# Set-up and experts' copies of a fused convolution, attention and mixture-of-experts kernel: the third norm's roots on VectorE, weights loaded by SyncE, copies paced

## The chip, the cores and the metric

The kernel runs on one core of a Trainium2 chip. The metric is the device time of one execution in microseconds (us), here as the median of three runs. The engines are named PE (TensorE), DVE (VectorE), ACT (ScalarE), POOL (GpSimd) and SP (SyncE, which issues DMAs and computes nothing). Each engine takes its instructions in order and waits on semaphores; DMAs are issued by SP, ACT or POOL and run beside them.

## The reference

The input x has 8 images of 56x56 positions with 256 channels. A convolution layer of 32 paths comes first, then an attention layer over the positions of each image, then a mixture of 8 experts of which each token uses two.

```python
def path(x, w1, b1, ..., v3):                    # 32 of these, each with D = 4 inner channels
    h = relu(bn(x @ w1 + b1, g1, be1, m1, v1))   # 256 -> 4
    h = conv3x3(h, w2, padding="SAME") + b2      # 4 -> 4
    h = relu(bn(h, g2, be2, m2, v2))
    h = h @ w3 + b3                              # 4 -> 256
    return relu(bn(h, g3, be3, m3, v3))          # bn: g * (h - m) * rsqrt(v + 0.001) + b

x = relu(sum(path(x, *w) for w in weights) + x)
t = tokens(x)
t = t + attention(layernorm(t))                  # 8 heads, linear in the keys and values
n = layernorm(t)
y = n
for e in range(8):                               # weights: softmax over the router, best two
    y = y + weight[:, e] * (gelu(n @ w1[e] + b1[e]) @ w2[e] + b2[e])
t = t + y
```

The change concerns the constants `g3`, `b3`, `m3`, `v3`, `be3` of the third norm, the 3x3 weights `W2`, and the copies of `w1`, `b1`, `w2` of the experts.

## The kernel before, in words

**Chunks and slots.** The 3136 positions of each image are cut into 7 chunks of 448 (`CH`), 56 chunks in all (`S`). The main loop runs over slots. In slot s TensorE computes the third convolution (`conv3_steps`, L625) of chunk s; beside it stand the first convolution of chunk s+2 (`conv1_steps`: transposes `tx` of the chunk's input `xi` at L260, then products with `W1s` at L271, then ACT writes `h1`), the 3x3 convolution of chunk s+1 (`spread_taps` copies shifted rows of `h1` into `R`, `conv2_steps` multiplies them with `W2t` at L307 and splits the result into `hi` and `lo`, which DMAs interleave into the tile `hl`), the layer norm of chunk s-1 (`end_steps`), and, from slot 8 on, the attention, routing and expert tiles of earlier chunks. `hl` has two buffers, `xi` has one.

**Order.** For PE, ACT and DVE the order of instructions is written out by hand: each part of a slot is a list of steps with weights or places between 0 and 1, and `issue` sorts all steps of a slot by place. conv3 gives 32 pairs of products in 16 steps of weight 0.7 and 8 sums of weight 0.9, spread over the whole slot. SP and POOL are not in that list: a scheduler puts their instructions in the order in which it expects them to become ready. A DMA of SP with nothing to wait for is so moved to the front of the program.

**Pacing.** `pair` keeps its latest product in `pace`. The scatters of rows (POOL) are given a dependency on `pace[0]`, that is on the last pair of conv3 that was placed before them, so that they are spread over the slot.

**The set-up.** Before slot 0 the constants are loaded and rearranged. `path_rows` loads each of the third norm's five vectors as a tile of 128 partitions x 64. POOL raises `v3` + 0.001 to the power -0.5 (L209). DVE makes the factor `g3` and the offset `b3`. `whole` copies each of them by four DMAs into a tile of 32 x 256, alternating between the queues of ACT and SP (L196). TensorE spreads `g3` over 128 partitions with the matrix `spread` (L373, `tp_g`), DVE multiplies `W3s` by it, four pairs of products (L380, L381, `tp_w`) place the result in `W3hl`, and `bias3` becomes `b3t` through L409 (`tp_b`). ACT loads `W2s` by 12 DMAs (L217), from which DVE makes `W2t`. Two chunks of conv1 and the first chunk of conv2 are computed among this. For chunk 0, ACT issues one of the three DMAs of `R` (L294) and the two of `hl` that take `lo` (L329).

**The experts' copies.** `copy_weights(e)` gathers the weights of expert e in a DRAM tensor `Wd` (three DMAs: two of 256 KB at L488 and a small one at L494), and `empty_rows(e)` writes an empty tile `pad` of 259 KB to the head of the expert's part of each of two DRAM tensors `regions` (L1296; POOL clears the tile at L1294). Both are called in slots 1 to 8, at the places 0.5 and 0.8:

```python
if 1 <= s <= E:
    work_of.append((0.5, 0.5, [(0.0, lambda: copy_weights(s - 1))]))
    work_of.append((0.8, 0.8, [(0.0, lambda: empty_rows(s - 1))]))
```

They depend on nothing that the slots compute, and SP's order places them where it will.

Of the kernel before, what the change touches and what calls it, by code (L numbers as in the profile page):

```python
# [8 lines left out]
F32 = mybir.dt.float32  # L9
BF16 = mybir.dt.bfloat16  # L10
I32 = mybir.dt.int32
F32R = mybir.dt.float32r
AF = mybir.ActivationFunctionType
ALU = mybir.AluOpType
# [7 lines left out]
SYNC = mybir.DependencyInfo(mybir.DependencyClass.Sync, mybir.DependencyReason.DATA)  # L22
# [3 lines left out]
def kernel(  # L26
# [24 lines left out]
    nc = tc.nc  # L51
    B, N, C = x.shape
# [6 lines left out]
    P = 128  # L59
    NF = C // P  # L60
# [36 lines left out]
    setup = setup_pool.__enter__()  # L97
# [10 lines left out]
    for g in range(NG):  # L108
        nc.scalar.dma_start(
            out=bn2s[32 * g : 32 * g + 32],  # L110
            in_=bn2[32 * g : 32 * g + 32].rearrange("(a e) k -> e a k", a=4),
# [24 lines left out]
    def group_mask(t, groups, size, value):  # L136

        nc.gpsimd.memset(t, value)
        nc.gpsimd.affine_select(
            out=t, in_=t, compare_op=ALU.is_ge, fill=0.0, base=0,  # L140
            pattern=[[-size, groups], [0, t.shape[2]]], channel_multiplier=1,
        )
        nc.gpsimd.affine_select(
            out=t, in_=t, compare_op=ALU.is_ge, fill=0.0, base=size - 1,
            pattern=[[size, groups], [0, t.shape[2]]], channel_multiplier=-1,
        )
# [34 lines left out]
        gather, ident.rearrange("q (p c) -> q c p", c=32), AX.X, ALU.add  # L181
    )


    CQ = C // 4

    def path_rows(src, name):
        t = setup.tile([P, CQ], F32, name=name)
        nc.sync.dma_start(out=t, in_=src.rearrange("p (q c) -> (p q) c", q=4))
        return t  # L190

    def whole(parts_of, name):
        t = setup.tile([NP, C], F32, name=name)
        for q in range(4):
            queue = nc.sync if q % 2 else nc.scalar
            queue.dma_start(out=t[:, q * CQ : (q + 1) * CQ], in_=parts_of[q : P : 4, :])  # L196
        return t

    v3 = path_rows(V3, "v3")
    g3 = path_rows(G3, "g3q")  # L200
    b3 = path_rows(B3, "b3q")
    m3 = path_rows(M3, "m3")
    be3 = path_rows(Be3, "be3")
    W3s = setup.tile([P, C], F32, name="W3s")
    nc.sync.dma_start(out=W3s, in_=W3.rearrange("p d c -> (p d) c"))
    nc.vector.tensor_scalar_add(v3, v3, BN_EPS)
    mhalf3 = setup.tile([P, CQ], F32, name="mhalf3")
    nc.gpsimd.memset(mhalf3, -0.5)
    nc.gpsimd.tensor_tensor(v3, v3, mhalf3, ALU.pow)  # L209


    path32 = setup.tile([P, GP, D], F32, name="path32")
# [1 line left out]
    W2s = setup.tile([3 * 32, NG, 3, D], F32, name="W2s")  # L214
    for dx in range(3):
        for g in range(NG):
            nc.scalar.dma_start(  # L217
                out=W2s[dx : 3 * 32 : 3, g],
                in_=W2[32 * g : 32 * g + 32].rearrange(
                    "q (dy dx o) -> dx q dy o", dy=3, dx=3  # L220
                )[dx],
            )
# [117 lines left out]

    path_mask = setup.tile([P, NP, D], F32, name="path_mask")
    group_mask(path_mask, NP, D, 1.0)
    nc.vector.tensor_mul(g3, g3, v3)
    nc.vector.tensor_sub(b3, b3, m3)
    nc.vector.tensor_mul(b3, b3, g3)
    nc.vector.tensor_add(b3, b3, be3)
    g3 = whole(g3, "g3")
    bias3 = whole(b3, "bias3")

    picks = setup.tile([P, 2, NQ, P], F32, name="picks")  # L350
    nc.gpsimd.memset(picks, 0.0)
# [18 lines left out]
    spread = setup.tile([NP, P], F32, name="spread")  # L370
# [112 lines left out]
    NTOK = B * N  # L483
    M = 2 * E + 1

    def copy_weights(e):
        for n, w in enumerate((w1, w2)):
            nc.sync.dma_start(  # L488
                out=Wd[e, :, n * NF * C : (n + 1) * NF * C].rearrange(
                    "p (f h) -> p f h", f=NF  # L490
                ),
                in_=w[e].rearrange("(f p) h -> p f h", p=P),
            )
        nc.sync.dma_start(out=Wd[e, :, 2 * NF * C :], in_=b1T[:, e * NF : (e + 1) * NF])  # L494

    regions = [
        tc.dram_tile([E * CAPR, ROW], F32, name=f"regions_{k}") for k in range(2)
# [1 line left out]
    Wd = tc.dram_tile([E, P, WROW], F32, name="Wd")  # L499
# [42 lines left out]
    for e in range(M):  # L542
# [6 lines left out]
        out=below, in_=below, compare_op=ALU.is_ge, fill=0.0, base=-1,  # L549
# [8 lines left out]
        out=earlier, in_=earlier, compare_op=ALU.is_ge, fill=0.0, base=-1,  # L558
# [13 lines left out]
    def unordered(ins, group, keep=()):  # L572

        tc.declare_no_dep(ins, group=group, keep=keep, reason="other rows")
# [95 lines left out]

    spilled, rs1s, kvs = {}, {}, {}
    G = KT * NH

    def inverse_root(v, y, h):

        nc.vector.tensor_scalar(y, v.bitcast(I32), 1, None, ALU.arith_shift_right)
        nc.vector.tensor_scalar(y, y, -1, 0x5F3759DF, ALU.mult, ALU.add)
        y = y.bitcast(F32)
        for _ in range(3):
            nc.vector.scalar_tensor_tensor(h, y, -0.5, v, op0=ALU.mult, op1=ALU.mult)  # L680
            nc.vector.tensor_mul(h, h, y)
            nc.vector.scalar_tensor_tensor(y, h, 1.5, y, op0=ALU.add, op1=ALU.mult)
        return y

    def end_steps(s):
        b, c = divmod(s, NCH)
# [58 lines left out]
        def variances():  # L745
# [28 lines left out]
            y = stat.tile([T, KT, NH + 1], I32, tag="root1", name=f"root1_{s}", bufs=1)  # L774
            h = stat.tile([T, KT, NH + 1], F32, tag="root2", name=f"root2_{s}", bufs=1)
            y = v["y"] = inverse_root(sd, y, h)
            nc.vector.tensor_mul(sd, sd, y)

# [133 lines left out]
    def attn_steps(a):  # L912
# [15 lines left out]
        def attend(k):  # L928

            ps = ps_mm.tile([T, C + 2 * E], F32, tag="mm", name=f"at_{a}_{k}")  # L930
            for f in range(NF):
                nc.tensor.matmul(  # L932
                    ps, tT[:, f, k * T : (k + 1) * T], tables_of[b][:, f, :],
                    start=(f == 0), stop=(f == NF - 1),
                )
            nc.vector.scalar_tensor_tensor(
                X[:, k, :], ps[:, :C], rs1[:, k : k + 1], X[:, k, :],
                op0=ALU.mult, op1=ALU.add,
            )
            late.append(lambda: nc.scalar.copy(lg[:, k, :], ps[:, C:]))  # L940
            if k:
                late.pop(0)()
            nc.vector.bn_stats(st[:, k, :], X[:, k, :])
            nc.vector.bn_aggr(mv[:, k, :], st[:, k, :])
            if k == KT - 1:
                nc.vector.tensor_scalar_add(rs2, mv[:, :, 1], LN_EPS)
                if alone:
                    y, h = (
                        stat.tile(
                            [T, KT, NH + 1], dt, tag=f"root{n}", name=f"root{n}_{a}_a", bufs=1  # L950
                        )[:, :, 0]
                        for n, dt in ((1, I32), (2, F32))
                    )
                    nc.vector.tensor_copy(rs2, inverse_root(rs2, y, h))
                else:
                    nc.gpsimd.tensor_tensor(rs2, rs2, mhalf[:T, :KT], ALU.pow)
# [43 lines left out]
    pace = []  # L1000
    before = {}

    def filled(b, ins):
        unordered(ins, "rows")
        unordered(ins, "tiles")
        tc.add_to_no_dep_group("rows", ins)
        before.setdefault(b, []).append(ins)
# [131 lines left out]
    def plan_steps(b):  # L1139
# [17 lines left out]
        def small(shape, tag, dtype=F32):  # L1157
            whole = [P, 2] + [NMAX if d == n else M if d == m else d for d in shape]
            if tag == "big":
                whole[2] = max(NMAX, M)  # L1160
            t = tables.tile(whole, dtype, tag=f"p_{tag}", name=f"{tag}_{b}")
            return t[tuple(slice(0, d) for d in [P, 2] + shape)]
# [129 lines left out]
    def empty_rows(e):  # L1292
        pad = slots.tile([P, 2, ROW], F32, tag="rows", name=f"pad_{e}", bufs=5)
        nc.gpsimd.memset(pad, 0.0)  # L1294
        for k in range(2):
            ins = nc.sync.dma_start(  # L1296
                out=regions[k][e * CAPR : e * CAPR + TR, :].rearrange("(h p) c -> p h c", p=P),
                in_=pad,
            ).ins
            filled(0, ins)  # L1300

    def take_rows(i):
# [185 lines left out]
    for s in range(S + A + 1):  # L1488
# [48 lines left out]
# [3 lines that stand above are left out]
# [65 lines left out]
```

## Time and profile before

| | |
|---|---|
| median of 3 runs | 3205.17 us (3203.22 to 3205.35) |
| the profiled execution's own time | 3181.84 us |
| its span in the profile | 3180.0 us |
| granted PE clock, mean | 0.964 |
| busy: PE, DVE, ACT, POOL | 2922.0, 2176.6, 1915.4, 1855.4 us |
| first product of conv3 (L625) | at 60.8 us |
| first pad and last pad issued by SP | at 24.9 and 75.5 us |
| DMAs of `Wd` issued by SP | at 13.5 to 72.6 us |

The span is the time between the first and the last instruction of one execution; the chain up to the first product of conv3 can be read in the timeline, where each row has the start, the duration, the engine (SPq and ACTq are the queues in which SP and ACT issue DMAs), the line, the operation with output and inputs, the count of merged instructions and, in brackets, the idle time before it and what ended it. Tile names stand without their numbers: `g<-g3q` is the DMA that fills the whole `g3`, `v` is `v3`, `h` is `h1` or `h2`, `c` any of the convolutions' results.

### The profile page before, as it was taken

Reading aid. Unit: us, or ns where it says so; the run is one execution under the profiler, and the core shown is the slowest. Engines: PE = TensorE matmul, PEld = TensorE weight load, DVE = VectorE, ACT = ScalarE, POOL = GpSimd, SP = SyncE. Lnnn points to the kernel's source line nnn. Section 1 sums busy time; section 2 is a strip of 40 time slices with the busy share of each in tenths; the row PEclk is TensorE's granted clock in tenths of the full one; section 3 lists DMA queues with packets and bytes.
Section 4 is the critical chain, followed back from the end, with each engine's and each line's share of the span. In section 5 each row is a group of like instructions: output and inputs, shape, how many; then the busy total and the mean of one; then the engine's idle time right before and its main releaser. Section 6 shows DMA issues by size and latency. Waiting matters only on the chain. (4 is left out here: it accounts for less than half of the span.)

```text
span 3180.0 us, 53655 instructions
## 1 busy us (share of the span) xinstructions
PE 2922.0 (92%) x16677; PEld 1664.3 (52%) x16677; DVE 2176.6 (68%) x5732; ACT 1915.4 (60%) x3827; POOL 1855.4 (58%) x1365
## 2 busy tenths in 40 slices
PE   5999888888999999999999999999999998898798
PEld 2333434334455555555555555555555545776687
DVE  3778877787878777776878687776777785444100
ACT  2676665555665666566666666566666664454355
POOL 3223254545566666757666675756764546677777
PEclk8999988898999999999999999999999999899999
DMA  8332343354456677566766667577665766898897
GB/s 173 117 108 83 104 130 116 113 152 149 135 161 187 161 196 194 162 178 186 195 170 174 189 174 194 158 185 196 173 191 152 193 164 169 189 265 219 200 228 179
DMA packets 322669, 537.53 MB, mean 169 GB/s; under 512 B 41152, under 2 KB 232784, under 8 KB 322384
## 3 DMA queue, kind: packets, MB, share of 16 engines
q1 hardware_dynamic: 238272, 429.85, 45.0%
q0 software_dynamic: 81984, 103.45, 17.8%
q8 instruction: 133, 2.18, 0.3%
q14 instruction: 152, 1.25, 0.1%
q10 hardware_dynamic: 2128, 0.81, 0.1%
HBM read 248.01 MB, written 192.55 MB: 139 GB/s over the span
## 5 line engine op out<-in xcount | busy, mean ns | idle before, releaser
L633 DVE SCALAR_TENSOR_TENSOR r<-c,nb,r 128x448 f32<-128x448 f32 x1792 | 1130.6, 676 | 433.1 <-ACT r L630 431.4
L630 ACT ACTIVATE r<-c,b3t 128x448 f32<-128x448 f32 x1792 | 1039.3, 635 | 338.9 <-PE c L625 333.4
L1405 POOL DMA_INDIRECT out_dram<-y,index x420 | 660.8, 1573 | 326.8 <-ACT y L1391 207.5
L625 PE MATMUL c<-hl,W3hl 64*128 64x448 f32 x3584 | 693.5, 429 | 48.2 <-ACT r L630 18.9
L1113 POOL DMA_INDIRECT regions<-pay,rrowi x448 | 429.2, 958 | 311.3 <-PE c L625 209.7
L646 PE MATMUL su<-r,gather 128*32 128x448 f32 x3584 | 554.6, 566 | 41.5 <-DVE r L633 38.6
L625 PEld LDWEIGHTS c<-hl,W3hl 64*128 64x128 f32 x3584 | 328.8, 189 | 480.6 <-issue 232.1
L1391 ACT ACTIVATE y<-py,rows 128x256 f32<-128x256 f32 x420 | 195.9, 475 | 471.8 <-PE py L1387 360.9
L1367 PE MATMUL ph<-eT,w 128*128 128x256 f32 x1680 | 451.3, 400 | 20.0 <-DMA w<-Wd 7.3
L1387 PE MATMUL py<-w,hT 128*128 128x256 f32 x1680 | 432.2, 382 | 0.0
L1367 PEld LDWEIGHTS ph<-eT,w 128*128 128x128 f32 x1680 | 304.6, 195 | 151.0 <-issue 50.9
L770 POOL TENSOR_TENSOR hsd<-hsd,half 112x36 f32<-112x36 f32 x49 | 304.5, 6215 | 67.1 <-DVE hsd L768 66.2
L1371 ACT ACTIVATE hT<-ph,w 128x256 f32<-128x256 f32 x420 | 197.1, 478 | 211.7 <-PE ph L1367 157.3
L1387 PEld LDWEIGHTS py<-w,hT 128*128 128x128 f32 x1680 | 291.6, 192 | 28.6
L932 PE MATMUL at<-tab,tT 128*112 128x272 f32 x896 | 262.7, 417 | 8.7 <-ACT r L630 6.6
L731 POOL TENSOR_TENSOR norm<-t,hmean 112x512 f32<-112x512 f32 x112 | 121.5, 1164 | 226.1 <-PE c L625 156.8
L646 PEld LDWEIGHTS su<-r,gather 128*32 128x32 f32 x3584 | 101.0, 109 | 245.2 <-DVE r L633 120.6
L1383 PE MATMUL py<-b2hl,own 128*128 128x256 f32 x420 | 179.4, 427 | 23.5 <-ACT y L1391 17.1
L932 PEld LDWEIGHTS at<-tab,tT 128*112 128x112 f32 x896 | 149.6, 181 | 86.4 <-issue 21.4
L1058 POOL TENSOR_TENSOR rq<-ebase,rq 112x8 f32<-112x8 f32 (+1 forms) x32 | 50.3, 1572 | 229.5 <-DVE rq L1057 229.1
L1383 PEld LDWEIGHTS py<-b2hl,own 128*128 128x128 f32 x420 | 79.7, 190 | 157.4 <-issue 45.2
L307 PE MATMUL c<-R,W2t 96*32 96x448 f32 x1344 | 149.9, 553 | 4.5 <-ACT r L630 4.5
(259 smaller groups left out, 3179.9 us busy)
## 6 DMA issues: line engine op xcount, KB each, us to landing
w<-Wd SPq DMA_DIRECT2D x210, 513.0 KB
rows<-regions SPq DMA_DIRECT2D x210, 259.0 KB
xi<-in_x_dram SPq DMA_DIRECT2D x56, 448.0 KB
hl<-hi SPq DMA_DIRECT2D x112, 224.0 KB
tTs<-u SPq DMA_DIRECT2D x56, 448.0 KB
ts<-t SPq DMA_DIRECT2D x56, 448.0 KB
tT<-tTs SPq DMA_DIRECT2D x56, 448.0 KB
X<-ts SPq DMA_DIRECT2D x56, 448.0 KB
```

The source lines that it names most:

```text
L625: product = nc.tensor.matmul(tiles[g][:, :CH], W3hl[rows, ab, cg, :], hl[rows, ab, :], start=True, stop=True)
L630: nc.scalar.activation(r, tiles[0][:, :CH], AF.Relu, bias=b3t[:, cg, 2 * ab : 2 * ab + 1])
L633: nc.vector.scalar_tensor_tensor(r, tiles[1][:, :CH], nb3[:, cg, 2 * ab + 1 : 2 * ab + 2], r, op0=ALU.max, op1=ALU.add,)
L646: nc.tensor.matmul(ps[32 * c4 : 32 * c4 + 32, :CH], gather, unit.pop((s, 4 * u + c4)), start=(ab == 0), stop=(ab == NQ - 1),)
L770: nc.gpsimd.tensor_tensor(sd, sd, half[:T, :].rearrange("q (k h) -> q k h", k=KT), ALU.pow)
L932: nc.tensor.matmul(ps, tT[:, f, k * T : (k + 1) * T], tables_of[b][:, f, :], start=(f == 0), stop=(f == NF - 1),)
L1113: ins = nc.gpsimd.indirect_dma_start(out=regions[n], out_offset=bass.IndirectOffsetOnAxis(ap=v["row_i"][:, (m - group[0]) * KT + k, n : n ...
L1367: nc.tensor.matmul(ps, w[:, f * C + hf * P : f * C + (hf + 1) * P], eT[:, f, :], start=(f == 0), stop=(f == NF - 1),)
L1371: nc.scalar.activation(hT[:, hf, :], ps, AF.Gelu, bias=w[:, 2 * NF * C + hf : 2 * NF * C + hf + 1])
L1383: nc.tensor.matmul(ps, own.to_broadcast([P, P]), b2hl, start=True, stop=False)
L1387: nc.tensor.matmul(ps, hT[:, f, h * P : (h + 1) * P], w[:, (NF + f) * C : (NF + f + 1) * C], start=False, stop=(f == NF - 1),)
L1405: ins = nc.gpsimd.indirect_dma_start(out=out_rows, out_offset=at, in_=y[:, h, :], in_offset=None, compute_op=ALU.add, **partial,).ins
```

## The change

- The root of the third norm is computed on DVE by `inverse_root`, which takes a first guess from the bits of the number and three Newton steps, 11 operations; the function stood further down and is moved up. The `pow` on POOL and its tile of exponents are gone.
- The four operations that make `g3` and `b3`, and the calls of `whole`, stand directly behind the root, not behind conv1 of the first two chunks.
- The DMAs of `whole` and of `W2s` are all issued by SP.
- The three DMAs of `copy_weights` and the two of `empty_rows` get a dependency on `pace[0]`, so SP issues them in the slots in which they are called.

```diff
@@ set-up
     def whole(parts_of, name):
         t = setup.tile([NP, C], F32, name=name)
         for q in range(4):
-            queue = nc.sync if q % 2 else nc.scalar
-            queue.dma_start(out=t[:, q * CQ : (q + 1) * CQ], in_=parts_of[q : P : 4, :])
+            nc.sync.dma_start(out=t[:, q * CQ : (q + 1) * CQ], in_=parts_of[q : P : 4, :])
         return t
...
     nc.vector.tensor_scalar_add(v3, v3, BN_EPS)
-    mhalf3 = setup.tile([P, CQ], F32, name="mhalf3")
-    nc.gpsimd.memset(mhalf3, -0.5)
-    nc.gpsimd.tensor_tensor(v3, v3, mhalf3, ALU.pow)
+    v3 = inverse_root(
+        v3, setup.tile([P, CQ], I32, name="root3"), setup.tile([P, CQ], F32, name="rest3")
+    )
+    nc.vector.tensor_mul(g3, g3, v3)
+    nc.vector.tensor_sub(b3, b3, m3)
+    nc.vector.tensor_mul(b3, b3, g3)
+    nc.vector.tensor_add(b3, b3, be3)
+    g3 = whole(g3, "g3")
+    bias3 = whole(b3, "bias3")
...
     for dx in range(3):
         for g in range(NG):
-            nc.scalar.dma_start(
+            nc.sync.dma_start(
                 out=W2s[dx : 3 * 32 : 3, g],
...
     path_mask = setup.tile([P, NP, D], F32, name="path_mask")
     group_mask(path_mask, NP, D, 1.0)
-    nc.vector.tensor_mul(g3, g3, v3)
-    nc.vector.tensor_sub(b3, b3, m3)
-    nc.vector.tensor_mul(b3, b3, g3)
-    nc.vector.tensor_add(b3, b3, be3)
-    g3 = whole(g3, "g3")
-    bias3 = whole(b3, "bias3")
@@ the experts' copies
+    def paced(ins):
+
+        tc.add_manual_dep(ins, pace[0].name, SYNC, reason="spread over the slot")
+        return ins
+
     def copy_weights(e):
         for n, w in enumerate((w1, w2)):
-            nc.sync.dma_start(
+            load = nc.sync.dma_start(
                 out=Wd[e, :, n * NF * C : (n + 1) * NF * C].rearrange(
...
-        nc.sync.dma_start(out=Wd[e, :, 2 * NF * C :], in_=b1T[:, e * NF : (e + 1) * NF])
+            paced(load.ins)
+        paced(
+            nc.sync.dma_start(out=Wd[e, :, 2 * NF * C :], in_=b1T[:, e * NF : (e + 1) * NF]).ins
+        )
@@ empty_rows
             ).ins
+            paced(ins)
             filled(0, ins)
```

The function that is moved up:

```python
def inverse_root(v, y, h):
    nc.vector.tensor_scalar(y, v.bitcast(I32), 1, None, ALU.arith_shift_right)
    nc.vector.tensor_scalar(y, y, -1, 0x5F3759DF, ALU.mult, ALU.add)
    y = y.bitcast(F32)
    for _ in range(3):
        nc.vector.scalar_tensor_tensor(h, y, -0.5, v, op0=ALU.mult, op1=ALU.mult)
        nc.vector.tensor_mul(h, h, y)
        nc.vector.scalar_tensor_tensor(y, h, 1.5, y, op0=ALU.add, op1=ALU.mult)
    return y
```

The order of instructions that follows: PE's is the same throughout, ACT loses 16 DMA issues, DVE gains 11 operations, and SP's differs only up to slot 8.

More of the change, by code (lines that the diff above doesn't have):

```diff
@@ L182, with inverse_root @@
     )
+    def inverse_root(v, y, h):
+        nc.vector.tensor_scalar(y, v.bitcast(I32), 1, None, ALU.arith_shift_right)
+        nc.vector.tensor_scalar(y, y, -1, 0x5F3759DF, ALU.mult, ALU.add)
+        y = y.bitcast(F32)
+        for _ in range(3):
+            nc.vector.scalar_tensor_tensor(h, y, -0.5, v, op0=ALU.mult, op1=ALU.mult)
+            nc.vector.tensor_mul(h, h, y)
+            nc.vector.scalar_tensor_tensor(y, h, 1.5, y, op0=ALU.add, op1=ALU.mult)
+        return y
     CQ = C // 4
@@ L672 @@
     G = KT * NH
[L674 to L683, printed above, removed]
     def end_steps(s):
```

## The prediction

> **What bounds the kernel now.** I read the page first (busy shares, slices), then the stage table of the first 100 us, then the timeline of the set-up and of one slot. The page gives 3180.0 us:
>
> ```profile
> PE   5999888888999999999999999999999998898798
> DMA  8332343354456677566766667577665766898897
> ```
>
> TensorE is busy nine tenths almost everywhere; the exception is the first slice (79.5 us), at five tenths, where the DMA engines are at eight. The change touches this slice and the eight slots after it, so only they are read further. The stage table (stage, busy us of PE, PEld, DVE, ACT, POOL, granted PE clock, DMA share, GB/s) compares a stretch of the set-up with a stretch of slots:
>
> ```profile
> 30.00:40.00 10.00, 5.02 (x13) 3.69 (x14) 2.69 (x5) 0.26 (x1) 0.53 (x1) 0.54 0.96 194
> 80.00:100.00 20.00, 18.59 (x122) 7.67 (x114) 14.10 (x23) 14.12 (x27) 0.00 (x0) 1.00 0.32 109
> ```
>
> In the set-up no compute engine is full, the clock is halved and the DMA engines are saturated; in the slots TensorE is at 93% and DMA has two thirds free. So the set-up is a chain of waits, and its end is the first product of conv3 (L625). In the timeline (start, duration, engine, line; in brackets the idle time and what ended it) that chain is:
>
> ```profile
> 4.30 8.20 ACTq L217 DMA_DIRECT2D W2s<-in_W_dram  x12
> 9.64 10.58 POOL L209 TENSOR_TENSOR v<-v,mhalf 128x64 f32<-128x64 f32 x1
> ...
> 14.94 0.53 SPq L87 DMA_DIRECT2D xi<-in_x_dram  x1
> ...
> 20.69 1.76 PE L260 MATMUL tx<-ident,xi 112*128 112x112 f32 x8 [2.93 <-DMA xi<-in_x_dram]
> ...
> 26.52 0.63 ACTq L294 DMA_DIRECT2D R<-h  x1
> 27.24 2.02 ACTq L196 DMA_DIRECT2D g<-g3q  x2
> 29.36 1.48 ACTq L196 DMA_DIRECT2D bias<-b3q  x2
> 30.88 0.26 ACT L371 COPY spread<-tp_mask 32x128 f32<-32x128 f32 x1 [4.43 <-issue]
> ...
> 34.05 1.19 PE L373 MATMUL tp_g<-g,spread 32*128 32x256 f32 x2 [8.26 <-DMA g<-g3q]
> ...
> 46.67 4.71 PE L307 MATMUL c<-R,W2t 96*32 96x448 f32 x24
> 54.12 1.33 SPq L329 DMA_DIRECT2D hl<-hi  x2
> 54.30 1.81 ACTq L329 DMA_DIRECT2D hl<-lo  x2
> 60.79 1.11 PE L625 MATMUL c<-hl,W3hl 64*128 64x448 f32 x4 [6.52 <-DMA hl<-lo]
> ```
>
> TensorE waits 8.26 us for g3: half of it sits on ScalarE's queue behind R, and lands among the experts' copies. It waits 6.52 us more for hl.
>
> **What the Trainium skill says.** "DMA: Bandwidth & Descriptors", section "Issuing engines are not separate DMA queues": issuing on several engines saves only the sequencer's time. The trace agrees that this time is real: 8.20 us for twelve 1.5 KB loads, in which ScalarE did nothing else. The same page, "Anatomy of one DMA — SWDGE (gpsimd) path": a semaphore wait is held on the issuing sequencer before dispatch, so a paced copy holds all behind it on SP. Its "Queues, rings and completion order": SP and ACT each own one row, descriptors are consumed in ring order. "TensorE: Matmul & The Clock Gate", section "What's actually happening": the clock is halved after about 3.4 us of idling. The trace agrees: conv2's 24 matmuls took 4.71 us here and 2.46 in slot 1.
>
> **The change part by part.** All landmarks are of this execution.
>
> 1. *The root on VectorE.* Removed: 10.58 us of POOL and a memset (0.14). Added: 11 VectorE operations of 128x64; the dependent ones of that size (L343 to L346) start 0.25 us apart, so 2.8 us. v3 is ready at 9.1, g3 and b3 at 12.8 instead of 21.1. W2t now stands behind them, but its data come later anyway. Nothing on POOL waited for the pow.
>
> 2. *Loads on SP.* ACT's queue keeps only bn2s, so conv1 of chunk 0 is about 6 us earlier; that is hidden, since chunk 1 waits for its xi. On SP the instruction order of the changed kernel puts W3s, then 12 W2s, then xi of chunk 1, then 4 g3 and 4 bias3. W2s can start near 6.3 us (its completion semaphores are free once xi of chunk 0, used at 6.04, has landed) and takes 8.2 as on ACT: xi is issued at 14.6, no earlier than the 14.94 of now. But the first Wd copies (512 KB) no longer stand ahead of it: xi of chunk 0 took 4.0 us from issue to use, this one 5.75. So the transposes start at 18.7, **2.0 us earlier**. From there to h1 written takes 5.75 as now: 24.45. g3 and bias3 are issued by 20.1 and, even with the 4.8 us that the last g3 part took in the crowd, have landed by 25. ACT issues its R (0.65) and copies spread at once, without 3.5 us of DMA issue ahead: g3's product can start at 25.5 instead of 34.05, **8.5 us earlier** (the 2.0 included).
>
> 3. *From there to conv2's end* I keep the 17.3 us (34.05 to 51.38): 42.9. R, issued at 24.5 into an empty queue, is long there. Behind it on SP now stand b2s, kw, kb, vw, vb and rwc, six issues of 0.6 us, done by 30; the first of them in use is rwc, after conv2. If the clock stays full here, since the 8.26 us idle is gone, up to 3.5 us less (4.71 against 2.46, and about 1.2 in the 381 products).
>
> 4. *hl of chunk 0.* SP was late for it: hi was ready at 52.6, issued at 54.12 after a lane wait for Wd. In the new order xi of chunk 3 stands ahead of hl on SP and waits for chunk 2's transposes (2.9 us after conv2, as now): xi at 45.8, hi issued by 47.5, lo on ACT from 44.8. Then xi's 459 KB and hl's 917 KB move together; at the 300 GB/s that the DMA engines gave from 55 to 61 us this takes 4.6 us from 46.0: 50.6. With a little overlap I take **50.3 against 60.76: 10.5 us** (8.5 from above and 2.0 here).
>
> 5. *Slot 0* begins in the same cold state: 0.
>
> 6. *The copies in slots 1 to 8.* Each slot gets 3 DMAs of Wd at 0.5 of the slot and 2 of pad at 0.8 on SP, 1.04 MB. DMA share in the slots is 0.2 to 0.5: bandwidth costs 0. Behind Wd on SP stand only tT and X (used seven slots later). Behind the pads stands hl of the next chunk, which is urgent. In slot 1:
>
> ```profile
> 116.33 1.79 PE L625 MATMUL c<-hl,W3hl 64*128 64x448 f32 x8
> 119.60 0.55 SPq L329 DMA_DIRECT2D hl<-hi  x1
> 122.24 0.60 SPq L329 DMA_DIRECT2D hl<-lo  x1
> 123.00:124.00 1.00, 1.00 (x12) 0.24 (x10) 0.71 (x3) 0.71 (x2) 0.00 (x0) 1.00 0.95 358
> 124.00:125.00 1.00, 1.00 (x9) 0.40 (x6) 1.00 (x2) 0.66 (x2) 0.00 (x0) 1.00 0.13 48
> 125.81 0.84 PE L625 MATMUL c<-hl,W3hl 64*128 64x448 f32 x4
> ```
>
> hl lands at 124.15 (48 KB left after 124) and is used at 125.81: 1.66 us of slack. The pads wait for the last pair placed before 0.8, pairs 24 and 25: conv3 has 16 double pairs of weight 0.7 and 8 sums of 0.9, so pair 24 stands at 0.769 and sum 5 at 0.81. These are the last products of the block at 116.33, done at 118.1, **before** hi is ready (119.57). The two issues (1.04 us) are over at 119.2; 530 KB at the 274 GB/s of 35 to 36 us (when pads moved) are through at about 121.2; hl then needs 2.6 us at 358 GB/s and its last issue is at 122.24 anyway: landing 124.2. Cost 0; bounds 0 to 0.5 us a slot (pads at the 119 GB/s of the worst crowd: 126.3). In slot 8 hi is ready before 0.8 and hl is held some 1.7 us, but the next product comes at 374.92, after an end near 372. POOL's last three pad memsets wait for earlier pads, after norm's scaling: the next POOL operation, norm's centring of the next chunk, is over ten us off.
>
> Sum: 10.5 us less, bounds 6.5 (xi no earlier, hl after xi) to 14 (clock). Nothing later changes order; TensorE's order is the same throughout, so the whole rest shifts. Against the execution: 3181.84 (span plus 1.84) becomes 3171.3. The median of the runs is 23.3 us higher; the same difference gives 3205.2 - 10.5 = 3194.7.
>
> **The rivals.**
> - *Gain at set-up, partly given back* (0.15): a measurement tells about 0.2% (6.4 us) from no change. If hl is late by 0.5 to 0.9 us in seven slots (4 to 6 us), or SP's single queue makes xi of chunk 1 as late as now and hl later (gain 4 to 6), the time is 3199 to 3203. For it: SP issues 16 more DMAs in the set-up (12 W2s, 2 g3, 2 bias3) at 0.6 us. Against: g3 is needed only when conv1 of chunk 1 is done, and that doesn't wait for SP after xi.
> - *Slower: SP's order in the slots* (0.07). The pads' wait stands ahead of hl in eight slots. It decides once hl lands over 1.66 us later; to be slower by over 6.4 us it must land 4.1 us later in each of seven slots (7 x 2.4 = 17 us lost): 3212. For it: a released pad after pair 27 (120.9) would shift all of SP by 1.4 us and the bytes by 2. Against: pair 25 by the weights, and even then only about 1 us a slot is lost, 3202.
> - *The move doesn't happen*: excluded by the instruction order, in which no Wd or pad stands before slot 1. *More than forecast*: with the clock warm, 3191.
>
> **How the numbers follow.** The forecast, set-up 7 to 14 us shorter and slots unchanged: 0.78, 3194.7, alone 3191 to 3198.5. The range takes in the give-back up to 3203. Faster 0.78, same 0.15, slower 0.07.
>
> **What would show it.** Right: L625 starts near 50 instead of 60.8, no wait for g3 in front of L373, spread copied right after R, DMA share under 0.7 from 30 to 45 us, slots 1 to 7 at 33.95 us each with Wd and pads in them, the rest shifted by one amount. Wrong: TensorE idle before L625 at the slots' starts, released by hl; W2s on SP ending after 16 us; a wait of the first conv3 products that falls on another tile.

## The result and the profile after

| | before | after |
|---|---|---|
| median of 7 runs each | 3205.35 us (3203.22 to 3218.32) | 3192.65 us (3186.59 to 3197.43) |
| ratio | | 0.9948, 95% interval 0.9931 to 0.9965 |
| profiled execution, span | 3180.0 us | 3192.3 us |
| first product of conv3 | 60.79 us | 52.91 us |

The kernel is faster, by 16.7 us (11.2 to 22.1) if the ratio is taken; the two medians differ by 12.7 us, for three of the seven runs of before (3210.59, 3212.47 and 3218.32 us) lie 5 us and more above the other four. I had said 10.5 us, at most 14. Two more comparisons below gave 12.7 and 12.4 by their ratios. The profiled executions are no guide to the total: that of before was shorter than all of its timed runs, that of after about average, so by their spans the change would be a loss. They have to be read stage by stage.

The page of after, busy tenths of PE and DMA in 40 slices of 79.8 us:

```profile
PE   6999888888999999999999999999999997887798
DMA  2543344344556666667665766667756666898897
```

In the first slice DMA falls from eight tenths to two; the copies now stand in slices two to five. The stage table of after (stage, busy us of PE, PEld, DVE, ACT, POOL, granted PE clock, DMA share, GB/s):

```profile
30.00:40.00 10.00, 7.08 (x30) 5.78 (x33) 5.58 (x12) 0.00 (x0) 0.00 (x0) 0.67 0.23 28
80.00:100.00 20.00, 18.46 (x100) 7.89 (x100) 15.03 (x25) 15.31 (x29) 2.06 (x2) 1.00 0.49 160
```

From 30 to 40 us the DMA share is 0.23, where it was 0.96, and the clock is still not full. The slots carry the copies (share 0.49 for 0.32) with PE as busy as before. The timeline of the set-up of after (start, duration, engine, line; in brackets the idle time before and what ended it):

```profile
7.66 7.71 SPq L233 DMA_DIRECT2D W2s<-in_W_dram  x12
...
12.89 0.23 DVE L192 SCALAR_TENSOR_TENSOR root<-rest,root 128x64 f32<-128x64 f32 x1
...
15.48 0.52 SPq L87 DMA_DIRECT2D xi<-in_x_dram  x1
16.10 2.79 SPq L206 DMA_DIRECT2D g<-g3q  x4
...
19.12 1.76 PE L276 MATMUL tx<-ident,xi 112*128 112x112 f32 x8 [7.91 <-DMA xi<-in_x_dram]
...
20.75 3.35 PE L287 MATMUL c<-xT,W1s 128*128 128x448 f32 x4
...
25.98 0.69 PE L383 MATMUL tp_g<-g,spread 32*128 32x256 f32 x2 [1.66 <-ACT spread L381]
...
28.88 1.06 PE L390 MATMUL tp_w<-W3h,picks 128*128 128x256 f32 x2
...
35.90 3.55 PE L419 MATMUL tp_b<-pdiv,b 32*128 32x8 f32 x16 [2.92 <-DVE b L414]
39.38 4.71 PE L323 MATMUL c<-R,W2t 96*32 96x448 f32 x24
...
46.01 1.25 ACTq L345 DMA_DIRECT2D hl<-lo  x2
47.01 0.34 SPq L87 DMA_DIRECT2D xi<-in_x_dram  x1
47.45 1.34 SPq L345 DMA_DIRECT2D hl<-hi  x2
...
52.91 1.12 PE L643 MATMUL c<-hl,W3hl 64*128 64x448 f32 x4 [5.93 <-DMA hl<-hi]
```

The wait for g3 is gone: `tp_g` now waits 1.66 us, for `spread`. The long waits left are 7.91 us for the input of chunk 1, which SP issues only behind the twelve W2s, and 5.93 us for `hl`. So one idle stretch of some 8 us has gone and another has come, earlier: before, the same transposes waited 2.93 us. Slot 1 of after, where the pads stand ahead of the next chunk's `hl`:

```profile
110.34 0.92 SPq L1303 DMA_DIRECT2D regions<-pad  x2
111.75 0.61 SPq L345 DMA_DIRECT2D hl<-hi  x1
...
114.40 0.61 SPq L345 DMA_DIRECT2D hl<-lo  x1
```

The pads are off SP at 111.26, half a microsecond before `hi` is issued. The last `hl` issue was at 122.24 before: it has moved by 7.84 us, just as the whole slot has.

### The profile page after: what moved, and what is told of

It is laid out like the page before. It is cut to its first block, busy times and chain, and to the rows that moved or that the text cites. A ratio compares the mean times of both kernels' runs of the same rounds, so it can differ in the third digit from the quotient of the medians.

```text
span 3192.3 us, 53679 instructions
## 1 busy us (share of the span) xinstructions
PE 2924.8 (92%) x16677; PEld 1663.9 (52%) x16677; DVE 2173.6 (68%) x5743; ACT 1919.8 (60%) x3827; POOL 1844.5 (58%) x1363
## 3 DMA queue, kind: packets, MB, share of 16 engines
q0 software_dynamic: 81984, 103.45, 17.8%
## 4 chain that ended last, share of the span: by engine, by line
PE 68%; DVE 10%; issue 4%; ACT 3%; POOL 3%; DMA 2%; another core or an unknown queue 0%; ACTq 0%; SPq 0%; POOLq 0%; DVEq 0%
PE c L643 12%; PE ph L1375 11%; PE su L664 11%; PE py L1395 9%; PE at L939 7%; PE kv L813 3%; DVE r L651 3%; PE te L1335 3%; PE c L323 2%; PE py L1391 2%; POOL hsd L777 2%; PE c L287 2%; ACT r L648 2%; PE tu L712 1%; PE tx L276 1%
## 5 line engine op out<-in xcount | busy, mean ns | idle before, releaser
L943 DVE SCALAR_TENSOR_TENSOR X<-at,rs,X 112x256 f32<-112x256 f32 x224 | 107.0, 478 | 122.4 <-PE at L939 60.8
L1339 ACT COPY eT<-te 128x512 f32<-128x512 f32 x210 | 123.5, 588 | 60.5 <-PE te L1335 40.6
```

## The experiments

Three theories stood at the start. **A**: the lead that the set-up gains is the whole effect; it goes through to the end and the rest is scatter. **B**: something after slot 8 gains another 4 to 9 us. Within the set-up, **crowd** (the copies made every transfer late) stood against **root and queue** (the late pow and ScalarE's queue did). Where the texts say lead, it is the distance of the first product of conv3 from that of the kernel before.

### The changed kernel again, twice

No edit.

> The changed kernel itself, unaltered, against the kernel before. In the two profiles the first product of conv3 stands at 52.9 us instead of 60.8, and the slots up to the eighth keep that lead of 7.9 to 8.2 us; the timed runs differ by some 12 to 17 us. Theory A: the lead of the set-up is the whole effect, and the rest is scatter between runs; then more runs give a difference near 8 us, a ratio of about 0.9975. Theory B: something after slot 8 is shorter too (copies of the experts' weights off the way of another transfer, a warmer clock), so that the difference stays near 15 us, a ratio of about 0.995, and the same stage shows a lead over the kernel before in every profile. Both expect the first product of conv3 at 52.9.

> The changed kernel once more, for the size of its gain. Its two profiles have the first product of conv3 at 52.9 and 51.0 us, those of the kernel before at 60.8 and 63.0: a lead of 9.9 us between the means; its timed runs were 16.7 (5.5 either way) and 12.7 us (4.5 either way) ahead. Theory A, the lead of the set-up is everything: conv3 again at 51 to 53, and a difference near 10 us, ratio 0.9962 to 0.9974. Theory B, some further gain of 4 to 6 us later in the kernel: ratio 0.9945 to 0.9958, and a stage after slot 0 that is shorter than in every profile of the kernel before.

Measured: 0.9960 (0.9946 to 0.9974) and 0.9961 (0.9946 to 0.9975), that is 12.7 and 12.4 us of medians of 3182.71 and 3180.43 us. First product of conv3 at 50.98 and 51.08. The first profile had it at 52.91: 16 products of the bias ran wholly at half clock there (3.55 us; 2.25 and 2.12 here), and `tp_g` stood 0.5 to 0.6 us later. The ratios decide nothing between A and B: the first lies between the two forecasts, which took the lead for 8 us, the second just below A's 0.9962 to 0.9974 and above B's 0.9958, and its interval holds values of both. What decides is in the stages, below.

### The kernel before again, twice

No edit. The second is timed against itself.

> The kernel before, unaltered, for a second profile of it. All five profiles with paced copies (the changed kernel twice, the delayed one, the pacing alone, the root with pacing) take 208.8 to 211.7 us from the first activation of u in slot 7 to that in slot 12; the one profile of the kernel before takes 214.4. Theory A (set-up alone, the rest is chance of the clock): the second profile of the kernel before takes 209 to 212 there, and its first product of conv3 stands at 59 to 61. Theory B (the pacing shortens slots 8 to 12 by some 4 us): it takes 214 to 215 again.

> The kernel before against itself, for the scatter of a timed comparison and for a third profile. If the comparison is fair, the ratio is 1 within 0.0015. The first product of conv3 is expected at 60 to 63.5. If it stands below 59, the lead of the set-up is smaller than the two profiles say; if above 63.5, it is larger, and the size that the timed runs gave is explained by the set-up.

Measured: the first product of conv3 stands at 63.02 and 65.53 us. The timeline of the second profile of before, the DMAs of `hl` and the product that waits for them:

```profile
54.49 2.71 SPq L329 DMA_DIRECT2D hl<-hi  x2
54.79 3.25 ACTq L329 DMA_DIRECT2D hl<-lo  x2
...
63.02 1.11 PE L625 MATMUL c<-hl,W3hl 64*128 64x448 f32 x4 [8.28 <-DMA hl<-lo]
```

and of the third:

```profile
55.75 2.40 SPq L329 DMA_DIRECT2D hl<-hi  x2
56.16 3.83 ACTq L329 DMA_DIRECT2D hl<-lo  x2
...
65.53 1.12 PE L625 MATMUL c<-hl,W3hl 64*128 64x448 f32 x4 [8.39 <-DMA hl<-lo]
```

Two issues of `lo` took 3.25 and 3.83 us, where they took 1.81 in the profile that I had, and PE waited 8.3 us instead of 6.5: among the copies this wait is not a constant, and the profile shown before the change is the shortest set-up of three. Both stand later than I had expected. The mean is 63.11 us, and the three of after give 51.66: **a lead of 11.5 us**. What these texts call slots 7 to 12, from the activation of `u` for chunk 7 to that for chunk 12, took 209.8 and 214.0 us, so the 214.4 of the first profile is no mark of this kernel, which goes against B. Two kernels below with paced copies took 214.2 there, and the one with early copies 210.6: pacing does not set this stretch. The kernel against itself gave 1.0009 (0.9996 to 1.0021).

### The lead given back

```diff
+            if s == 0:
+                idle = setup.tile([P, CH], F32, name="idle")
+                for _ in range(16):
+                    nc.vector.tensor_tensor(idle, h2, h2, ALU.add)
             nc.vector.tensor_copy(hi, h2)
```

> The changed kernel with sixteen additions of 128x448 on VectorE put in front of the rounding of h2 in chunk 0, to no purpose but to hold up hl by about 8 us; everything after it is as changed. At 0.5 us each they push the first product of conv3 from 52.9 to 60 or 61, where the kernel before has it. Theory A (the lead of the set-up is the whole effect): no difference left to the kernel before, a ratio of 0.999 to 1.001. Theory B (a further gain of 5 to 9 us after the set-up, from where the copies now are): a ratio of 0.997 to 0.998 in spite of the delay.

Its timeline:

```profile
43.25 10.50 DVE L341 TENSOR_TENSOR idle<-h 128x448 f32<-128x448 f32 x16 [4.97 <-ACT h L332]
...
45.34 0.34 SPq L87 DMA_DIRECT2D xi<-in_x_dram  x1
...
54.08 1.21 SPq L349 DMA_DIRECT2D hl<-hi  x2
```

Measured: the additions took 10.5 us, conv3 began at 58.33, ratio 0.9984 (0.9969 to 0.9999), 5.1 us. Neither forecast of the ratio is met as written, since both took before's conv3 for 60.8; from the mean of 63.1 the lead left is 4.8 us, and 5.1 were measured. Against the changed kernel of the same session the lead fell by 7.35 us and the time rose by 7.6 (7.5 by the medians). That is what theory A says; B, with a further gain of 5 us at least, would be at 9.8 us or more, where the interval ends (9.9).

A by-product: here the input of chunk 3, issued at 45.34, had long landed when `hl` was issued, and `hl` took 4.25 us from its first issue (54.08) to its use, not 6.9.

### One part of the change alone

The pacing alone, put on the kernel before:

```diff
+    def paced(ins):
+        tc.add_manual_dep(ins, pace[0].name, SYNC, reason="spread over the slot")
+        return ins
...
+            paced(load.ins)
```

> The kernel before with one of the three edits alone: the experts' copies and pads wait for their slots, while the third norm's root stays on GpSimd, and W2s and half of g3 and bias3 on ScalarE's queue. Theory 'crowd' (the copies were what made every transfer of the set-up late): xi of chunk 1 is issued near 12 us and its transposes start near 17.8, h is written near 23, g3's product starts near 28.7 (ScalarE still issues its g3 and bias3 parts after R), and the first product of conv3 near 55.5: 5 us of the 7.9 are gained by the pacing alone, ratio about 0.998. Theory 'root and queue' (the late pow and ScalarE's queue were what counted): g3's product stays after 32 us and conv3 after 59, ratio 0.9995 to 1.

The changed kernel without the pacing:

```diff
     def paced(ins):
-        tc.add_manual_dep(ins, pace[0].name, SYNC, reason="spread over the slot")
         return ins
```

> The changed kernel without the pacing: the root on VectorE and all loads on SP stay, but the experts' copies and pads go out as soon as SP reaches them, in the set-up. Theory 'crowd': g3, R and hl again land among the copies; g3's product near 27 to 30 and the first product of conv3 at 57 to 60, so that nearly all of the lead is gone (ratio 0.9985 to 1). Theory 'root and queue': the lead comes from g3 being early and from its issues being off ScalarE, conv3 at 53 to 55, ratio 0.996 to 0.9975. For slots 7 to 12 theory A expects 209 to 212 us, theory B 214 to 215, since the copies are early as in the kernel before.

Measured: pacing alone 54.55 us and 0.9977 (0.9967 to 0.9987); without it 54.33 us and 0.9968 (0.9958 to 0.9979). Each half alone gains 8.6 to 8.8 us of the 11.5, so they overlap. Pacing alone meets "crowd" and goes a little past it; the kernel without pacing meets "root and queue". Both causes were there, and each remedy takes away the same wait for g3. The timeline of pacing alone:

```profile
27.26 1.22 PE L373 MATMUL tp_g<-g,spread 32*128 32x256 f32 x2 [6.16 <-ACT spread L371]
...
54.55 1.11 PE L633 MATMUL c<-hl,W3hl 64*128 64x448 f32 x4 [6.63 <-DMA hl<-hi]
```

`tp_g` no longer waits for g3, but for `spread`, which ScalarE still copies only behind its g3 and bias3 issues; it stands 6.8 us earlier than in before. The timeline of the kernel without pacing shows what pacing adds:

```profile
26.18 0.69 PE L383 MATMUL tp_g<-g,spread 32*128 32x256 f32 x2 [1.65 <-ACT spread L381]
...
45.80 2.21 SPq L345 DMA_DIRECT2D hl<-hi  x2
46.73 1.44 ACTq L345 DMA_DIRECT2D hl<-lo  x2
...
54.33 1.11 PE L642 MATMUL c<-hl,W3hl 64*128 64x448 f32 x4 [7.15 <-DMA hl<-lo]
```

`tp_g` is 0.6 us later than the mean of the changed kernel, and `hl`, again among copies, takes 8.5 us from its first issue to its use instead of 6.9.

### Who issues what

W2s and half of the g3 and bias3 parts back on ScalarE:

```diff
-            nc.sync.dma_start(out=t[:, q * CQ : (q + 1) * CQ], in_=parts_of[q : P : 4, :])
+            queue = nc.sync if q % 2 else nc.scalar
+            queue.dma_start(out=t[:, q * CQ : (q + 1) * CQ], in_=parts_of[q : P : 4, :])
...
-            nc.sync.dma_start(
+            nc.scalar.dma_start(
                 out=W2s[dx : 3 * 32 : 3, g],
```

> The changed kernel with W2s and half of the g3 and bias3 parts given back to ScalarE's queue; the root is on VectorE, the copies are paced. ScalarE's queue now has the first g3 part, which waits for VectorE until about 13.8 us, ahead of the twelve W2s and of the table load. Theory 'SP is needed': W2s go out from 16 to 24 us, conv1 of chunk 0 follows near 27, that of chunk 1 near 33 to 35, g3's product near 36, and the first product of conv3 near 63, later than in the kernel before: ratio 1.0005 to 1.001. Theory 'only the crowd counts': W2s are needed first at conv2, so little is lost, conv3 at 52 to 55 and the ratio near 0.998.

Measured: conv3 at 60.49, ratio 0.9988 (0.9976 to 1.0000). The mechanism of "SP is needed" is in its timeline:

```profile
12.97 1.46 ACTq L207 DMA_DIRECT2D g<-g3q  x2
14.52 1.20 ACTq L207 DMA_DIRECT2D bias<-b3q  x2
15.76 7.82 ACTq L234 DMA_DIRECT2D W2s<-in_W_dram  x12
23.61 1.28 ACT L280 ACT_TABLE_LOAD   x1 [23.61 <-DMA W2s<-in_W_dram]
```

All of ScalarE's work stands behind g3, so conv1 of chunk 0 begins after 25 us. It is not slower than before, as I had expected, for the two reasons already seen: conv3 came 2.5 us sooner than I reckoned, and before stands at 63.1.

W2s alone back on ScalarE, the g3 and bias3 parts on SP:

```diff
-            nc.sync.dma_start(
+            nc.scalar.dma_start(
                 out=W2s[dx : 3 * 32 : 3, g],
```

> The changed kernel with W2s alone back on ScalarE's queue. The kernel with this and hl on ScalarE has conv3 at 46.65, the one with hl alone there at 50.41, the changed kernel at 51 to 53. If the two edits add up, this one has g3's product near 22.6 to 23, as there, and the first product of conv3 at 48 to 49.5; ratio 0.9945 to 0.996. If the clock was what made the other kernel quick (conv2 4.16 us there), it stands at 49.5 to 51.

Measured: conv3 at 46.88, ratio 0.9962 (0.9948 to 0.9977). Its timeline:

```profile
12.22 0.33 SPq L87 DMA_DIRECT2D xi<-in_x_dram  x1
...
17.43 1.70 PE L276 MATMUL tx<-ident,xi 112*128 112x112 f32 x8
...
19.00 1.98 PE L287 MATMUL c<-xT,W1s 128*128 128x448 f32 x4
...
22.79 0.69 PE L383 MATMUL tp_g<-g,spread 32*128 32x256 f32 x2 [1.70 <-ACT spread L381]
...
25.36 0.59 PE L390 MATMUL tp_w<-W3h,picks 128*128 128x256 f32 x2
...
46.88 1.12 PE L643 MATMUL c<-hl,W3hl 64*128 64x448 f32 x4 [5.65 <-DMA hl<-hi]
```

The input of chunk 1 leaves SP 3 us earlier, and the set-up is 4.8 us shorter than the mean of the changed kernel. So one part of the change, W2s on SP, is a loss in the set-up, in the one profile there is: it keeps SP from `xi`. Only 1.4 of the 4.8 us are the earlier start of the transposes. Most of the rest is the clock: here TensorE idles before conv1 of chunk 0 and not before these transposes, the four products of conv1 take 1.98 us and not 3.35, and a pair of `tp_w` 0.59 us and not 1.06 (granted clock 1.00 from 23 to 28 us; 0.70 from 23 to 26 and 0.57 from 28 to 32 in the first profile of the changed kernel). From the transposes to `tp_g` this kernel so needs 1.4 us less, from there to conv2's result 1.7 less. I had thought of the clock only for conv2, which took 4.71 us as before, and it went better than my 48 to 49.5. The timed runs can't tell this kernel from the changed one (medians 3167.23 and 3168.88 us in the same session).

All four `hl` DMAs of chunk 0 on ScalarE, first with W2s on SP as changed, then with W2s on ScalarE too:

```diff
-                queue = nc.scalar if s == 0 and v % 2 else nc.sync
+                queue = nc.scalar if s == 0 else nc.sync
```

> The changed kernel with all four hl DMAs of chunk 0 issued by ScalarE; SP issues only xi of chunk 3 there. My step 4 said hl waits for SP's turn behind xi of chunk 3, and that xi's bytes and hl's then share the DMA engines. If SP's turn is the price, hi is issued near 45.5 instead of 47.5 and the first product of conv3 starts at 50.5 to 51 instead of 51 to 53 (a gain of 1.5 to 2.5 us, ratio near 0.9955). If the bytes are the price (hl's 917 KB take 4 to 6 us from the first issue whatever the queue), it starts within 0.7 us of the changed kernel.

> The changed kernel with W2s back on ScalarE's queue and all four hl DMAs of chunk 0 there too. My step 2 was late by 1.4 us because W2s on SP ended at 15.4, ahead of xi of chunk 1. With W2s on ScalarE (4.3 to 12.5 us) xi of chunk 1 is issued by about 11, and conv1 of chunk 0 ends at 17.8, which becomes the limit: transposes of chunk 1 near 17.8, g3's product 24 to 25 instead of 25.4 to 26, and with hl on ScalarE the first product of conv3 at 49 to 50.5. Ratio near 0.995. If ScalarE's queue with W2s delays the table load and the copies of chunk 0 more than that, the transposes of chunk 1 stay at 19 and only the gain of hl is left.

Measured: 50.41 us and 0.9963 (0.9944 to 0.9982); 46.65 us and 0.9944 (0.9923 to 0.9965). The timeline of the first:

```profile
43.50 0.59 ACTq L345 DMA_DIRECT2D hl<-hi  x1
...
45.44 0.62 ACTq L345 DMA_DIRECT2D hl<-lo  x1
...
50.41 1.12 PE L643 MATMUL c<-hl,W3hl 64*128 64x448 f32 x4 [5.28 <-DMA hl<-lo]
```

conv2's result was read at the same time as in the changed kernel's second profile (42.31 and 42.24). The first `hi` went out 2.0 us sooner (45.53 there), and the product came 0.6 us sooner. From the first of the four issues to the product it takes 6.9 us here and in all three profiles of after, 6.6 with W2s alone on ScalarE and 6.8 with both. SP's turn was not the price; the bytes and a fixed part are. The second kernel did better than my 49 to 50.5, as W2s alone on ScalarE had (46.65 against 46.88): from conv2's result on, `hl` on ScalarE saves 0.5 us there (7.99 against 8.47), but that result came 0.25 us later.

### A kernel from the findings

```diff
-        nc.sync.dma_start(
+        queue = nc.scalar if s == 1 else nc.sync
+        queue.dma_start(
             out=X, in_=x[b, c * CH : (c + 1) * CH, :].rearrange("(k q) c -> q k c", q=T)
...
     nc.scalar.copy(spread, tp[:NP, :P])
+    W2s = setup.tile([3 * 32, NG, 3, D], F32, name="W2s")
...
```

The input of chunk 1 and, after `spread`, the 12 loads of W2s go by ScalarE; the products that make W2t follow those that make the bias's operand. `hl` stays on ScalarE.

> A kernel made from the findings: paced copies, root on VectorE, hl of chunk 0 on ScalarE, xi of chunk 1 issued by ScalarE right behind chunk 0's copies, and W2s, which nothing needs before conv2, loaded by ScalarE only after spread; W2t is multiplied while TensorE does the 16 products of the bias. If the first chunk's xi was the next limit, xi is issued near 9.3, the transposes of chunk 1 start near 13.2 instead of 17.6, g3's product (now held by g3 itself, ready at 12.8, issued by 15.3) near 18.5 instead of 22.6, and the first product of conv3 at 42 to 43.5: another 3 to 4.5 us under the kernel with W2s and hl on ScalarE, ratio 0.9930 to 0.9945. If g3's transfer or W2t is late (g3 after 21, W2t after 31), conv3 stands at 44.5 to 46.5 and nothing measurable is gained.

Measured: conv3 at 43.54, a lead of 19.6 us over before, ratio 0.9952 (0.9936 to 0.9968), which is less than the 0.9930 to 0.9945 that I had expected, though the interval reaches there. The steps of the set-up fell near where they were expected; only that `tp_g` waited for `spread`, not for g3:

```profile
12.74 0.99 PE L258 MATMUL tx<-ident,xi 112*128 112x112 f32 x8 [1.55 <-DMA xi<-in_x_dram]
...
18.62 1.21 PE L374 MATMUL tp_g<-g,spread 32*128 32x256 f32 x2 [1.67 <-ACT spread L363]
...
43.54 1.12 PE L642 MATMUL c<-hl,W3hl 64*128 64x448 f32 x4 [6.49 <-DMA hl<-lo]
```

It beats the kernel before. Its set-up is 8.1 us shorter than that of the changed kernel, but the two medians of the same session, 3167.84 and 3168.88, are too close to say that the total is shorter too.

## Why the prediction was right or wrong

All comparisons together, each kernel's lead (against the mean of before, 63.11 us) beside what the timed runs gave:

| kernel | lead, us | timed gain, us |
|---|---|---|
| changed, first comparison | 10.2 | 16.7 ± 5.5 |
| changed, second | 12.1 | 12.7 ± 4.5 |
| changed, third | 12.0 | 12.4 ± 4.6 |
| lead given back | 4.8 | 5.1 ± 4.8 |
| pacing alone | 8.6 | 7.3 ± 3.2 |
| without pacing | 8.8 | 10.2 ± 3.3 |
| W2s and half of g3, bias3 on ScalarE | 2.6 | 3.8 ± 3.8 |
| W2s on ScalarE | 16.2 | 12.1 ± 4.6 |
| hl on ScalarE | 12.7 | 11.8 ± 6.1 |
| both | 16.5 | 17.8 ± 6.7 |
| from the findings | 19.6 | 15.3 ± 5.1 |

(Timed gain: one minus the ratio, times the median of before in that session; ± is half the interval.) Only the first row's interval leaves out its own lead (it begins at 11.2), and it holds the mean lead of the changed kernel, 11.5. Theory A holds to what these runs can tell: neither the stretch to chunk 7 (step 6 below) nor that from chunk 7 to chunk 12 is shorter in each profile of after than in every one of before. From one activation of `u` to the next, two single slots are: one by 0.3 us, and one (47.8 to 47.9 us against 44.6, 44.7 and 47.7) that takes 47.4 to 47.9 us in the other kernels with paced copies. The three comparisons of the changed kernel, weighted by the inverse squares of their half-intervals, give 13.6 ± 2.8 us.

Step by step, with means over three profiles of each kernel:

| | before | after | forecast | measured |
|---|---|---|---|---|
| transposes of chunk 1 | 21.11 | 18.84 | -2.0 | -2.3 |
| `tp_g` | 34.04 | 25.60 | -8.5 | -8.4 |
| from `tp_g` to conv2's result read by ScalarE | 18.52 | 17.33 | 0 | -1.2 |
| from there to the first product of conv3 | 10.55 | 8.73 | -2.0 | -1.8 |
| sum of the last three rows | | | -10.5 | -11.5 |

- **Step 1, right.** The root's eleven operations ran from 9.77 to 13.12, g3 and b3 were ready at 14.04, 1.2 us later than I said, which cost nothing.
- **Step 2, right, by two errors that cancel.** W2s started at 7.66 (7.28 in a later profile) and not 6.3, so `xi` left at 15.48 instead of 14.6, but landed in 3.6 us instead of 4.0, and 5.75 us from the transposes to `h1` held to the hundredth in this profile. What I did not see is that W2s had better stayed on ScalarE: I compared SP's `xi` with the 14.94 of before, not with what SP could have done.
- **Step 3, mis-sized by 1.2 us.** "I keep the 17.3 us" took one execution for all. In the three profiles of before it was 17.4, 18.1 and 20.1, in those of after 18.2, 16.9 and 16.9. conv2 stayed cold in all three of after (4.71 us), so the bound of 3.5 us from a warm clock was not reached. I had reckoned that the clock could stay full since the 8.26 us of idle before `tp_g` was gone, and had called the earlier conv1 of chunk 0 hidden. But it opens a new idle stretch of 7.9 to 8.4 us before the transposes of chunk 1, and the clock was at half from 20 to 22 us in all three profiles of after. What a full clock is worth here the kernel with W2s on ScalarE shows.
- **Step 4, right in its difference by luck, wrong in both its ends.** I had `lo` issued from 44.8, moved the bytes from 46.0 at 300 GB/s in 4.6 us, and took 0.3 us off: 5.5 us from the first issue to the product. It is 6.9. The stage table of after, one microsecond each, shows what was left out:

```profile
46.00:47.00 1.00, 0.98 (x6) 0.63 (x4) 0.00 (x0) 0.00 (x0) 0.00 (x0) 0.50 0.00 0
47.00:48.00 1.00, 0.00 (x0) 0.00 (x0) 0.46 (x3) 0.71 (x4) 0.00 (x0) 0.50 0.71 253
...
51.00:52.00 1.00, 0.00 (x0) 0.00 (x0) 0.00 (x0) 0.00 (x0) 0.00 (x0) 0.50 0.99 316
52.00:53.00 1.00, 0.09 (x2) 0.12 (x2) 0.00 (x0) 0.00 (x0) 0.00 (x0) 0.50 0.06 21
```

  Issued at 46.01, no byte moves before 47; the last arrive just after 52, and the product starts at 52.91. The bytes (1.40 MB with `xi` and `b2hl`) took about 5 us, 280 GB/s, near the 300 that I used; the 0.3 us of overlap did not come, and some 0.6 us from the last byte to the product were missing from the sum. The time without bytes, before and after them, is nearly 2 us. The Trainium skill, "DMA: Bandwidth & Descriptors", section "Anatomy of one DMA — SWDGE (gpsimd) path", gives a DMA a fixed part of about 2.0 us besides its bytes, for that other path; the trace agrees in size, but over half of it lies ahead of the first byte, where the page puts most of it behind the last. The other end was too low as well: the wait for `hl` in before was 6.5 us in the profile I had and 8.3 and 8.4 in the next two.
- **Step 5, right.** From the first product of conv3 to the activation of `u` for chunk 0: 36.0, 35.6 and 35.9 us before, 36.0, 36.0 and 35.4 after.
- **Step 6, right.** From that activation to the one for chunk 7: 242.1, 241.5 and 241.2 us before, 241.8, 241.5 and 241.1 after, with the copies in.
- **Which step failed.** In the sum it is step 3: a term of 0 that measured -1.2 us, because one execution of before, whose set-up is 2.3 us shorter than the mean of three and 4.7 shorter than the longest, stood for all. With it the lead is 11.5 us and not 10.5, which does not reach 16.7. The step that failed beyond that is the bound: my 14 us is built from bounds of the steps alone (3.5 us for a warm clock). It leaves out the scatter of timed runs, though the rivals' part itself says that a measurement cannot tell less than 6.4 us from no change, and 10.5 and 6.4 would have reached 16.9. Of the 5.2 us between 11.5 and 16.7 no stage shows any; 4.0 are the distance of the ratio from the medians, with the three long runs of before, and two repeats, 12.7 and 12.4, did not keep them. Whether it was chance alone stays open.

The rivals that were to take something away did not come: nothing was given back in the slots, and SP's order there cost nothing. "More than forecast" came in the first comparison, but not by its cause: conv2 stayed cold.

## What to carry to other kernels

Before pricing a wait among crowded transfers, take it from more than one execution: here it varied by 2 us between executions of one kernel. Give a forecast's range the scatter of the measurement besides the bounds of its steps. Count for each transfer on the path a fixed part besides bytes over rate, here nearly 2 us. When loads move to another queue, ask what that queue could have issued earlier without them, not only whether it is later than today. When a wait of TensorE is removed, look where its next long wait will stand: here the idle stretch only moved forward, and the products behind it ran at half clock as before.

## What the runs showed of the hardware

- **Which queue issued did not matter to `hl`, what landed beside it did.** `hl` took 6.9 us from first issue to use by SP and ACT together and by ACT alone, with the input of chunk 3 moving beside it; 4.25 us when that had landed before. Beside it 1.40 MB moved in about 5 us, 280 GB/s; without it 0.93 MB in about 2.6 us, some 350 GB/s. The Trainium skill says the first half of this in "DMA: Bandwidth & Descriptors", section "Issuing engines are not separate DMA queues". Holding that input back until `hl` has landed was not tried.
- **The same wait can cost different amounts of cold clock.** Some 450 us into the kernel TensorE waits for the same operand of a sum in both kernels. Timeline of before:

```profile
450.28 2.29 PE L646 MATMUL su<-r,gather 128*32 128x448 f32 x4 [3.46 <-DVE r L633]
...
454.63 3.81 PE L806 MATMUL kv<-norm 112*128 112x129 f32 x16
```

  and of after:

```profile
442.17 2.29 PE L664 MATMUL su<-r,gather 128*32 128x448 f32 x4 [3.44 <-DVE r L651]
...
446.53 2.76 PE L813 MATMUL kv<-norm 112*128 112x129 f32 x16
```

  The waits differ by 0.02 us; behind them the sixteen products of `kv` take 3.81 us in one and 2.76 in the other, as the half clock lasts longer: the granted clock is 0.50 from 454 to 458 us in before, and 0.75 from 446 to 450 in after. The Trainium skill, "TensorE: Matmul & The Clock Gate", section "What's actually happening", describes a free-running window of about 3.4 us, by which it would depend on when in the window the wait falls; no trace here shows the window itself.
- **Times scatter with the granted clock.** The stretch from `u` of chunk 7 to that of chunk 12 took 208.8 to 211.7 us in ten of the fourteen profiles here, at a granted clock of 0.92 to 0.94, and 214.0 to 214.4 us in four, at 0.90, though PE's instructions in it are the same in all kernels. Whole runs go the same way: among 32 runs of before in one session, from 3175 to 3200 us, the longer tend to be those with the lower granted clock (0.959 to 0.971; correlation -0.74, about 1.4 us for each 0.001). Single spans so scatter by more than this change is worth.
